# Attention values with the query on the output rows, half of the probabilities transposed on VectorE, and x parked in DRAM

## The chip, the core and the metric

The kernel runs on one core of a Trainium2 chip. The metric is the device time of one execution in microseconds, as the median of several executions. All arithmetic is in 32-bit floats. A core has TensorE (PE, matrix products into PSUM), VectorE (DVE), ScalarE (ACT), GpSimd (POOL) and SyncE (SP). In this kernel POOL, SP and ACT also issue DMA transfers. Each engine works through its own instructions in order; semaphores order the engines among one another.

## The reference, cut to what matters

x is 32 batches of 32 tokens with 512 features. Four layers each add their result to x; the last one takes most of the time:

```python
x = x + einsum('bct,bcd->bdt', x, weights[condition])                 # layer 0: mix tokens
x = x + einsum('bsi,oi->bso', x, W) + low_rank(x, lora_A, lora_B)*.5   # layer 1
x = x + einsum('bsi,boi->bso', x, weight[adapter_ids])                 # layer 2
# layer 3: attention, 32 query heads, 8 key heads, head size 128
q, k, v = x @ Wq.T, x @ Wk.T, x @ Wv.T
q, k = rope(rmsnorm(q)), rope(rmsnorm(k))
k_all = concat(k_cache[block_table], k); v_all = concat(v_cache[block_table], v)  # 512 + 32 keys
probs = softmax(where(valid, q @ k_all.T / sqrt(128), -1e30))
x = x + (probs @ v_all) @ Wo.T
```

Each batch has 512 cached keys (16 pages of 32, gathered by a table) and 32 new ones.

## The kernel before, in words

**First part.** Layers 0 to 2 run in tiles of 128 rows (four batches, eight tiles `t`). The running x stays in SBUF in `xs` to the end of the kernel. The projections follow: 12 chunks `c` of 512 output columns (8 of q, 2 of k, 2 of v) times 8 tiles, four 128-deep matmuls each (L295). q and k are normed, rotated (L315 to L341), turned by 32x32 blocks on DVE (L348) and stored by SP to `q_d` and `k_d`; v goes by way of ACT to `v_d`. The output weights `wo` (8 MB) are loaded by SP in four transfers during chunks 3 to 6. They have head size on the partitions: `wo[:, h, :]` is the block of head `h`.

**Attention.** A unit is a batch `b` and a key head `g`: 256 units, in the order of b and then g. Its four query heads times 32 tokens fill the 128 partitions. Four units of a batch are a quad. The order of all five engines' instructions is written out by hand in one loop over steps `n`; what follows lists the stages of a unit and the step at which each stands.

- Scores, step n: two matmuls against 288 and 256 keys (L673, L674) into one PSUM tile of two banks, which has a single buffer. DVE then adds the mask, takes each row's minimum and writes SBUF (`pr`, L680), which releases the PSUM tile.
- Exponential, step n: ACT raises `pr` and sums each row in `den` (L687).
- Division, step n+1: DVE takes 1/den (L692) and multiplies the 512 cached columns (L696). ACT does that of the 32 new columns into `pq` (L700).
- Flip, step n+2: four PE transposes (L707) turn the probabilities so that keys lie on the partitions, and ACT copies them out of PSUM into `pt` (L709).
- Values, step n+3: four matmuls with the value page as the stationary operand and `pt` as the moving one (L743), so that the output has head size on the partitions and queries along the columns.
- Once per quad: the four units' new-key probabilities are transposed together (L731, ACT copy L733), and four 32-row products per quad add the new values (L755, eight instructions). DVE copies the quad's output to `ot` (L765). The output PSUM tile takes four banks and has one buffer.
- Late units: the first unit of a quad, from batch 4 on and but for one (55 in all), takes another way. ACT divides it (L694), and DVE turns it with sixteen transposes of 32x128 each (L721), four in each of the steps n+3 to n+6. Its values follow at n+7.

**Output projection.** Batch tile `t` gives 32 blocks (L777, one head each), which are spread over the 32 steps of the next tile by the list `SHARE`: in steps 32 to 255 most have one, some two or none. Then DVE adds `xs` (L785) and SP stores. The last tile's blocks come at the end.

**Loads.** At g = 0 of batch b SP loads the new keys, the queries and the 16 key pages of batch b+1; at g = 4 POOL loads its 16 value pages. Both fill the buffers of batch b-1. The last two v projections (`FILL = 2`) are interleaved with the first steps of attention.

## Time and profile before

| what | value |
|---|---|
| median of 3 runs | 1284.76 us (1284.72 to 1284.89) |
| the profiled execution, its time | 1285.19 us |
| its span in the trace | 1283.5 us |
| PE busy | 1264.7 us, 99% |
| DVE busy | 873.9 us, 68% |
| ACT busy | 604.9 us, 47% |
| POOL busy | 377.2 us, 29% |
| granted TensorE clock | 1.0 throughout |
| first score matmul, score matmul of step 32, of step 255 | 427.15, 508.78 and 1242.78 us |

In the profile an instruction is named by its line, its engine and its operation, and the tiles that it writes and reads stand as `out<-in`. A fp32 matmul appears as two instructions, a PE transpose as one. A group's columns are its busy time, the mean duration of one in ns, and the idle time of the engine just before, with what ended it. Matmuls are pipelined and their ends are modelled, so a matmul's cost is better read from the start of one to the start of the next than from its duration. A wait of PE can show in the weight load (PEld) that comes ahead of the matmul.

### The profile page before, as it was taken

The page shows a single profiled execution, that of the slowest core. Times are in us where ns is not written, and L with a number is a line of the kernel's source. Part 1 is how long each engine was busy: PE and PEld are TensorE (multiplying, and loading weights), DVE is VectorE, ACT ScalarE, POOL GpSimd, SP SyncE. Part 2 cuts the span into 40 slices and gives each one's busy share as a digit, 9 for nine tenths or more (in the row PEclk, how much of TensorE's full clock was granted, in tenths as well). Part 3 has the DMA queues.
Part 4 walks back from the last instruction along what each step waited for, and adds up shares of the span by engine and source line. Part 5 has one row for each costly group of instructions (what it writes and reads, how often), then busy time and mean ns, then how long its engine had stood idle before and what let it go on. Part 6 is the DMA issues. An engine that isn't in the chain of part 4 may idle for free.

```text
span 1283.5 us, 23176 instructions
## 1 busy us (share of the span) xinstructions
PE 1264.7 (99%) x6284; PEld 827.9 (65%) x6284; DVE 873.9 (68%) x2515; ACT 604.9 (47%) x1625; POOL 377.2 (29%) x618
## 2 busy tenths in 40 slices
PE   8999999999999999999999999999999999999998
PEld 5444444444444688777777777777777777777774
DVE  3333767787881265688778778778877877887770
ACT  1232555555653466445445445545545544544540
POOL 2301533333342034223322333223322332222400
PEclk9999999999999999999999999999999999999999
DMA  8985755565458389866777586696677667758700
GB/s 335 426 341 182 203 134 174 172 180 166 118 144 236 122 234 240 222 181 188 180 216 199 157 207 188 167 237 185 194 196 195 193 175 203 207 152 217 192 25 9
DMA packets 176515, 246.69 MB, mean 192 GB/s; under 512 B 26209, under 2 KB 145377, under 8 KB 170114
## 3 DMA queue, kind: packets, MB, share of 16 engines
q1 hardware_dynamic: 147810, 163.25, 43.3%
q0 software_dynamic: 24832, 67.27, 20.2%
q10 hardware_dynamic: 3744, 14.68, 3.5%
q8 instruction: 52, 0.85, 0.3%
q14 instruction: 77, 0.63, 0.2%
HBM read 217.84 MB, written 27.26 MB: 191 GB/s over the span
## 4 chain that ended last, share of the span: by engine, by line
PE 89%; DVE 7%; DMA 2%; issue 1%; SPq 1%; ACT 0%; POOL 0%; DVEq 0%
PE qkv L295 26%; PE f_ps L777 18%; PE o_ps L743 16%; PE s_ps L673 8%; PE s_ps L674 7%; PE p_ps L707 6%; DVE pt L721 3%; PE o_ps L755 2%; DVE pr L680 2%; DMA wa<-in_w_adapt_dram 2%; PE adapt L483 2%; DVE pr L696 1%; PE base L463 1%; PE pn_ps L731 1%; PE base L464 0%
## 5 line engine op out<-in xcount | busy, mean ns | idle before, releaser
L184 POOL DMA_DIRECT2D vt<-in_v_cache_dram x480 | 240.7, 502 | 561.4 <-PE o_ps L743 409.8
L295 PE MATMUL qkv<-wq,x3t 128*128 128x512 f32 x768 | 331.8, 593 | 0.0
L680 DVE CUSTOM_DVE_ANT_0 pr<-s_ps,mask 128x544 f32<-128x544 f32 x256 | 185.5, 725 | 192.6 <-PE s_ps L674 187.1
L743 PE MATMUL o_ps<-pt,vt 128*128 128x128 f32 x2048 | 273.9, 277 | 9.2 <-DVE pt L721 9.1
L721 DVE STREAM_TRANSPOSE pt<-pr 32x128 f32<-32x128 f32 x880 | 265.8, 302 | 14.2
L743 PEld LDWEIGHTS o_ps<-pt,vt 128*128 128x128 f32 x2048 | 253.1, 192 | 22.0 <-DVE pt L721 17.6
L295 PEld LDWEIGHTS qkv<-wq,x3t 128*128 128x128 f32 x768 | 145.3, 190 | 183.2 <-issue 183.1
L709 ACT COPY pt<-p_ps 128x512 f32<-128x512 f32 x201 | 117.8, 586 | 302.8 <-PE p_ps L707 302.8
L777 PE MATMUL f_ps<-wo,ot 128*128 128x512 f32 x512 | 257.3, 605 | 0.0
L687 ACT ACTIVATE pr<-pr,low 128x544 f32<-128x544 f32 x256 | 192.1, 750 | 104.7 <-DVE low L680 103.2
L673 PE MATMUL s_ps<-kt,qt 128*128 128x288 f32 x512 | 170.4, 415 | 0.4 <-DVE low L680 0.4
L339 POOL TENSOR_TENSOR ra<-ra,rs 128x512 f32<-128x512 f32 x80 | 101.6, 1271 | 228.5 <-DVE rs L333 153.8
L673 PEld LDWEIGHTS s_ps<-kt,qt 128*128 128x128 f32 x512 | 92.1, 190 | 97.0 <-issue 77.2
L341 ACT ACTIVATE ra<-ra,rinv 128x128 f32<-128x128 f32 x320 | 102.2, 390 | 107.1 <-POOL ra L339 105.5
L674 PE MATMUL s_ps<-kt,qt 128*128 128x256 f32 x512 | 152.4, 379 | 0.2 <-issue 0.2
L707 PE MATMUL p_ps<-ident,pr 128*128 128x128 f32 x804 | 121.0, 273 | 0.0
L674 PEld LDWEIGHTS s_ps<-kt,qt 128*128 128x128 f32 x512 | 97.2, 190 | 27.4 <-issue 0.6
L707 PEld LDWEIGHTS p_ps<-ident,pr 128*128 128x128 f32 x804 | 99.9, 141 | 21.1 <-ACT pn L733 1.8
L777 PEld LDWEIGHTS f_ps<-wo,ot 128*128 128x128 f32 x512 | 82.3, 190 | 37.5 <-issue 30.6
L696 DVE TENSOR_SCALAR pr<-pr,rden 128x512 f32<-128x512 f32 x201 | 98.3, 489 | 7.2
L317 DVE TENSOR_REDUCE ss<-sq 128x4 f32<-128x512 f32 x80 | 53.8, 675 | 49.4 <-ACT sq L315 49.0
L700 ACT ACTIVATE pq<-pr,rden 128x32 f32<-128x32 f32 x256 | 78.7, 307 | 0.0
(91 smaller groups left out, 822.6 us busy)
## 6 DMA issues: line engine op xcount, KB each, us to landing
vt<-in_v_cache_dram POOLq DMA_DIRECT2D x512, 128.0 KB, 4.0
kt<-in_k_cache_dram SPq DMA_DIRECT2D x512, 128.0 KB, 3.9
wa<-in_w_adapt_dram SPq DMA_DIRECT2D x32, 1024.0 KB, 11.7
q_d<-st SPq DMA_DIRECT2D x256, 64.0 KB, 1.8
qt<-q_d SPq DMA_DIRECT2D x32, 512.0 KB, 5.8
wq<-in_w_qkv_dram ACTq DMA_DIRECT2D x10, 1024.0 KB, 5.3
wo<-in_w_o_dram SPq DMA_DIRECT2D x4, 2048.0 KB
k_d<-st SPq DMA_DIRECT2D x64, 64.0 KB, 2.0
```

Of the source, the lines that this page charges most:

```text
L184: self.eng.dma_start(out=out, in_=row)
L295: nc.tensor.matmul(ps, x3[:, k, :], w[:, k, :], start=(k == 0), stop=(k == KC - 1),)
L673: nc.tensor.matmul(ps[:, first:L], q, kt4[:, :N_LOW, g, :], start=True, stop=True)
L674: nc.tensor.matmul(ps[:, L : first + LT], q, kt4[:, N_LOW:, g, :], start=True, stop=True)
L680: nc.vector.tensor_tensor_reduce(pr, ps[:, first : first + LT], mask, -SCALE, 3.0e38, ALU.add, ALU.min, low)
L687: nc.scalar.activation(pr, pr, AF.Exp, bias=low, scale=-1.0, accum_out=den)
L696: nc.vector.tensor_scalar(pr[:, :L], pr[:, :L], rden, None, ALU.mult)
L707: nc.tensor.transpose(pp[:, c, :], pr[:, c * P : (c + 1) * P], ident)
L709: nc.scalar.copy(pt, pp)
L721: nc.vector.transpose(pt0s[b, g][j * S : (j + 1) * S, :, i * S : (i + 1) * S], blocks[:, :, j, :])
L743: nc.tensor.matmul(po[:, u, :P], vt[:, c, g * D : (g + 1) * D], pt[:, c, :], start=(c == 0), stop=False,)
L777: nc.tensor.matmul(pfs[t], ots[t, h // HALF][:, h % HALF, :], wo[:, h, :], start=(h == 0), stop=(h == HQ - 1),)
```

## The change

- Values are computed with the probabilities stationary and the value page moving, so that the output has queries on the partitions. The division therefore moves to the end of a quad: the exponentials stay undivided, and `keep` takes four reciprocals, multiplies the quad's 128x512 output from PSUM by them on DVE, and turns it by 32x32 blocks on DVE into `ot`.
- The rows of `ot` now hold (query head within the key head, d mod 32) and its columns' blocks (key head, d div 32). `wo` is loaded in that order, in 16 transfers to 32 partitions each in place of 4 to 128.
- The first quad of every batch takes no PE transposes. Each of its four units is turned by one DVE transpose of 128x512 in 32x32 blocks (`turn`, at g = 3 and 4 of the batch). Sixteen copies of 32x512 (`place`) then move the blocks to the right quarter of the partitions, four in each of the steps that start seven after the batch's first. Of each four, ACT makes 2, 2, 2, 4 for batches 0 to 2 and 1, 1, 1, 3 afterwards, and DVE the rest.
- The second quad of every batch is flipped on PE as before. The second quad's values come first: values of the batch's units 4 to 7 at the steps 7 to 10 after the batch's first, those of 0 to 3 at 11 to 14. The loop runs 7 steps beyond the last unit.
- ACT copies the new columns undivided. The late way is gone.
- x is stored to DRAM by POOL after the first part, and its SBUF is given back; the last addition loads a 256 KB tile of it by SP.
- Four v projections instead of two are interleaved, at steps 0, 1, 3 and 5. Value pages are loaded at g = 7 in place of 4, and the output blocks start three steps later, with heads 16 to 31 first.

```diff
-FILL = 2
+FILL = 4
+    x_d = dram.tile([NT, P, HID], F32, name="x_d")
...
+    nc.gpsimd.dma_start(out=x_d.rearrange("t p d -> p t d"), in_=xs)
+    first_part.close()
...
+    w_o4 = w_o.rearrange("(k d) (g r) o -> r k d g o", d=S, r=REP)
...
-            nc.sync.dma_start(out=wo[:, hs, :], in_=w_o[:, hs, :])
+            r = c - 3
+            for k in range(D // S):
+                nc.sync.dma_start(
+                    out=wo[r * S : (r + 1) * S].rearrange("d (g k) o -> d g k o", g=HK)[:, :, k, :],
+                    in_=w_o4[r, k],
+                )
...
+        nc.scalar.activation(
+            pr, pr, AF.Exp, bias=low, scale=-1.0, accum_out=dens[quad][:, u : u + 1]
+        )
+        nc.scalar.copy(news_p[quad][:, u, :], pr[:, L:])
...
+    def turn(b: int, us):
...
+        for u in us:
+            nc.vector.transpose(
+                turned[b][:, :, u, :, :].rearrange("p j c s -> p c j s"),
+                prs[b, 0].pop(u)[:, :L].rearrange("p (c j s) -> p c j s", j=P // S, s=S),
+            )
+    def place(b: int, i: int, on_act: int):
...
+        for j in range(P // S):
+            dst = placed[b][j * S : (j + 1) * S, :, :, i * S : (i + 1) * S]
+            src = turned[b][i * S : (i + 1) * S, j, :, :, :]
+            dst, src = (a.rearrange("p u c s -> p (u c) s") for a in (dst, src))
+            if j < on_act:
+                nc.scalar.copy(dst, src)
+            else:
+                nc.vector.tensor_copy(dst, src)
...
+        pt = pts.pop((b, g)) if q else placed[b][:, u, :, :]
         for c in range(L // P):
             nc.tensor.matmul(
                 po[:, u, :P],
+                pt[:, c, :],
                 vt[:, c, g * D : (g + 1) * D],
-                pt[:, c, :],
...
+        nc.vector.reciprocal(rden, dens.pop((b, q)))
+        o = tp.tile([P, QUAD, D], F32, tag="os", name=f"os_{b}_{q}", bufs=1)
+        nc.vector.tensor_tensor(
+            o, po[:, :, :P], rden.unsqueeze(2).to_broadcast([P, QUAD, D]), ALU.mult
+        )
+        nc.vector.transpose(
+            ots[t, q][:, :, j * S : (j + 1) * S],
+            o.rearrange("p u (k d) -> p (u k) d", d=S),
+        )
...
-        t, i = divmod(n - BT * HK, BT * HK)
+        t, i = divmod(n - 3 - BT * HK, BT * HK)
...
+    LAG = 7
+    ON_ACT = [[2, 2, 2, 4], [1, 1, 1, 3]]
+    FILLS = {0: NT - 4, 1: NT - 3, 3: NT - 2, 5: NT - 1}
...
-                if ahead_b and g == 4:
+                if g == 7 and 1 <= b < B - 1:
...
+            if 2 <= n < N + 2 and units[n - 2][1] >= QUAD:
+                flip(*units[n - 2])
+            if n < N:
+                exponentials(*scored)
+            if n in FILLS:
+                projected(NCH - 1, FILLS[n], 2)
+            if n < N and g in (3, 4):
+                turn(b, (0, 1) if g == 3 else (2, 3))
+            if n >= LAG and (n - LAG) % HK < QUAD:
+                bm, i = divmod(n - LAG, HK)
+                place(bm, i, ON_ACT[bm + 1 >= BT][i])
+            if n >= LAG:
+                bv, i = divmod(n - LAG, HK)
+                values(bv, (i + QUAD) % HK)
```

More of the change, by code (lines that the diff above doesn't have):

```diff
@@ L93, in cond_resid_kernel @@
     nc.vector.tensor_copy(pm, pm_m)
-    xs = const.tile([P, NT, HID], F32, name="xs")
-    intp = ctx.enter_context(ExitStack())
-    ii = intp.enter_context(tc.tile_pool(name="a_ii", bufs=1, side="right")).tile(
-        [P, N_INT], I32, name="ii"
-    )
+    first_part = ctx.enter_context(ExitStack())
+    xip = first_part.enter_context(tc.tile_pool(name="a_xi", bufs=1, side="right"))
+    xs = xip.tile([P, NT, HID], F32, name="xs")
+    ii = xip.tile([P, N_INT], I32, name="ii")
     nc.sync.dma_start(out=ii, in_=ints)
@@ L615, in cond_resid_kernel @@
             projected(0, NT - 1, 2)
-    intp.close()
+    nc.gpsimd.dma_start(out=x_d.rearrange("t p d -> p t d"), in_=xs)
+    first_part.close()
     flips.close()
@@ L632, in cond_resid_kernel @@
         if 3 <= c < 7:
-            hs = slice((c - 3) * HQ // 4, (c - 2) * HQ // 4)
-            nc.sync.dma_start(out=wo[:, hs, :], in_=w_o[:, hs, :])
+            r = c - 3
[4 more added lines that the diff above has]
+                )
         if c == (HQ + HK) // REP:
@@ L658, in cond_resid_kernel, with quad_of @@
     ots = {}
-    prs, pos = {}, {}
+    dens, news_p, prs, pos = {}, {}, {}, {}
     first = L - N_LOW * PSIZE
-    def late(b: int, g: int):
-        return g % QUAD == 0 and BT <= b and (b, g) != (B - 1, QUAD)
+    def quad_of(b: int, g: int):
+        return b, g // QUAD
     def scores(b: int, g: int):
@@ L676, in scores @@
         )
-        pr = tp.tile([P, LT], F32, tag="pr0" if late(b, g) else "pr", name=f"pr_{b}_{g}", bufs=2 if late(b, g) else 3)
+        pr = tp.tile([P, LT], F32, tag="pr", name=f"pr_{b}_{g}", bufs=4)
         low = tp.tile([P, 1], F32, tag="low", name=f"low_{b}_{g}", bufs=4)
@@ L685, in exponentials @@
     def exponentials(b: int, g: int, pr, low):
-        den = tp.tile([P, 1], F32, tag="den", name=f"den_{b}_{g}", bufs=4)
-        nc.scalar.activation(pr, pr, AF.Exp, bias=low, scale=-1.0, accum_out=den)
-        return b, g, pr, den
-    def divide(b: int, g: int, pr, den):
-        rden = tp.tile([P, 1], F32, tag="rden", name=f"rden_{b}_{g}", bufs=4)
-        nc.vector.reciprocal(rden, den)
-        if late(b, g):
-            nc.scalar.activation(pr[:, :L], pr[:, :L], AF.Copy, scale=rden)
-        else:
-            nc.vector.tensor_scalar(pr[:, :L], pr[:, :L], rden, None, ALU.mult)
-        quad = (b, g // QUAD)
-        if g % QUAD == 0:
-            prs[quad] = tp.tile([P, QUAD, S], F32, tag="pq", name=f"pq_{b}_{g}")
-        nc.scalar.activation(prs[quad][:, g % QUAD, :], pr[:, L:], AF.Copy, scale=rden)
-        return b, g, pr
@@ L703, in flip @@
-    def flip(b: int, g: int, pr):
+        quad, u = quad_of(b, g), g % QUAD
+        if u == 0:
+            dens[quad] = tp.tile([P, QUAD], F32, tag="den", name=f"den_{b}_{g}", bufs=4)
+            prs[quad] = {}
+            news_p[quad] = tp.tile([P, QUAD, S], F32, tag="pq", name=f"pq_{b}_{g}")
+        nc.scalar.activation(
+            pr, pr, AF.Exp, bias=low, scale=-1.0, accum_out=dens[quad][:, u : u + 1]
+        )
+        nc.scalar.copy(news_p[quad][:, u, :], pr[:, L:])
+        prs[quad][u] = pr
@@ new lines, in cond_resid_kernel @@
+    turned, placed = {}, {}
+    def turn(b: int, us):
+        if 0 in us:
+            turned[b] = tp.tile(
+                [P, P // S, QUAD, L // P, S], F32, tag="turned", name=f"turned_{b}", bufs=1
+            )
[5 more added lines that the diff above has]
+    def place(b: int, i: int, on_act: int):
+        if i == 0:
+            placed[b] = tp.tile(
+                [P, QUAD, L // P, P], F32, tag="placed", name=f"placed_{b}", bufs=1
+            )
[7 more added lines that the diff above has]
+                nc.vector.tensor_copy(dst, src)
@@ L705, in flip @@
+    pts = {}
+    def flip(b: int, g: int):
+        pr = prs[quad_of(b, g)].pop(g % QUAD)
         pp = ps_p.tile([P, L // P, P], F32, tag="p", name=f"p_ps_{b}_{g}")
@@ L707, in flip, with flip_new, values @@
             nc.tensor.transpose(pp[:, c, :], pr[:, c * P : (c + 1) * P], ident)
-        pt = tp.tile([P, L // P, P], F32, tag="pt", name=f"pt_{b}_{g}")
-        nc.scalar.copy(pt, pp)
-        return b, g, pt
-    pt0s = {}
-    def turn_part(b: int, g: int, pr, i: int):
-        if i == 0:
-            pt0s[b, g] = tp.tile([P, L // P, P], F32, tag="pt0", name=f"pt0_{b}_{g}", bufs=1)
-        blocks = pr[i * S : (i + 1) * S, :L].rearrange("p (c j k) -> p c j k", j=P // S, k=S)
-        for j in range(P // S):
-            nc.vector.transpose(
-                pt0s[b, g][j * S : (j + 1) * S, :, i * S : (i + 1) * S], blocks[:, :, j, :]
-            )
-    pns = {}
-    def flip_new(b: int, g: int):
-        quad = prs.pop((b, g // QUAD))
-        pnp = ps_p.tile([P, P], F32, tag="p", name=f"pn_ps_{b}_{g}")
-        nc.tensor.transpose(pnp, quad.rearrange("p u s -> p (u s)"), ident)
-        pns[b, g // QUAD] = tp.tile([P, P], F32, tag="pn", name=f"pn_{b}_{g}")
-        nc.scalar.copy(pns[b, g // QUAD], pnp)
-    def values(b: int, g: int, pt):
+        pts[b, g] = tp.tile([P, L // P, P], F32, tag="pt", name=f"pt_{b}_{g}")
+        nc.scalar.copy(pts[b, g], pp)
+    pns = {}
+    def flip_new(b: int, q: int):
+        pnp = ps_p.tile([P, P], F32, tag="p", name=f"pn_ps_{b}_{q}")
+        nc.tensor.transpose(pnp, news_p.pop((b, q)).rearrange("p u s -> p (u s)"), ident)
+        pns[b, q] = tp.tile([P, P], F32, tag="pn", name=f"pn_{b}_{q}", bufs=3)
+        nc.scalar.copy(pns[b, q], pnp)
+    def values(b: int, g: int):
         vt, vn = vts[b], vns[b]
         q, u = divmod(g, QUAD)
-        if (b, q) not in pos:
+        if u == 0:
             pos[b, q] = ps_o.tile([P, QUAD, L], F32, tag="o", name=f"o_ps_{b}_{g}")
         po = pos[b, q]
+        pt = pts.pop((b, g)) if q else placed[b][:, u, :, :]
         for c in range(L // P):
@@ L749, in values @@
             )
-        if u == (0 if late(b, q * QUAD) else QUAD - 1):
+        if u == QUAD - 1:
             pn = pns.pop((b, q))
@@ L754, in values @@
                 r = slice(i * S, (i + 1) * S)
-                nc.tensor.matmul(po[:, i, :P], vn[r, q, :], pn[r, :], start=False, stop=True)
-            return b, q
-        return None
+                nc.tensor.matmul(po[:, i, :P], pn[r, :], vn[r, q, :], start=False, stop=True)
+            keep(b, q)
     def keep(b: int, q: int):
@@ L762, in keep, with finish @@
         t, j = divmod(b, BT)
-        if j == 0:
+        if (t, q) not in ots:
             ots[t, q] = bp.tile([P, HALF, P], F32, tag="ot", name=f"ot_{t}_{q}")
-        nc.vector.tensor_copy(
-            ots[t, q][:, :, j * S : (j + 1) * S].rearrange("d (u r) s -> d u r s", u=QUAD),
-            po[:, :, :P].rearrange("d u (r s) -> d u r s", r=REP),
-        )
-    pfs = {}
-    def finish(t: int, hs):
-        for h in hs:
-            if h == 0:
+        rden = tp.tile([P, QUAD], F32, tag="rden", name=f"rden_{b}_{q}")
+        nc.vector.reciprocal(rden, dens.pop((b, q)))
+        o = tp.tile([P, QUAD, D], F32, tag="os", name=f"os_{b}_{q}", bufs=1)
+        nc.vector.tensor_tensor(
+            o, po[:, :, :P], rden.unsqueeze(2).to_broadcast([P, QUAD, D]), ALU.mult
+        )
+        nc.vector.transpose(
+            ots[t, q][:, :, j * S : (j + 1) * S],
+            o.rearrange("p u (k d) -> p (u k) d", d=S),
+        )
+    pfs, x3s = {}, {}
+    BLOCKS = list(range(HALF, HQ)) + list(range(HALF))
+    def finish(t: int, ns):
+        for n in ns:
+            h = BLOCKS[n]
+            if n == 0:
                 pfs[t] = ps_p.tile([P, HID], F32, tag="f", name=f"f_ps_{t}")
+                x3s[t] = tp.tile([P, HID], F32, tag="x3", name=f"x3_{t}", bufs=1)
+                nc.sync.dma_start(out=x3s[t], in_=x_d[t])
             nc.tensor.matmul(
@@ L780, in finish @@
                 wo[:, h, :],
-                start=(h == 0),
-                stop=(h == HQ - 1),
-            )
-            if h == HQ - 1:
-                nc.vector.tensor_tensor(xs[:, t, :], xs[:, t, :], pfs.pop(t), ALU.add)
-                nc.sync.dma_start(out=out[t * P : (t + 1) * P, :], in_=xs[:, t, :])
+                start=(n == 0),
+                stop=(n == HQ - 1),
+            )
+            if n == HQ - 1:
+                x3 = x3s.pop(t)
+                nc.vector.tensor_tensor(x3, x3, pfs.pop(t), ALU.add)
+                nc.sync.dma_start(out=out[t * P : (t + 1) * P, :], in_=x3)
     SHARE = [1, 2] * 5 + [1] + [1, 1, 1, 0] * 5 + [1]
     def share(n: int):
-        t, i = divmod(n - BT * HK, BT * HK)
+        t, i = divmod(n - 3 - BT * HK, BT * HK)
         if 0 <= t < NT - 1 and i < len(SHARE):
@@ L799, in cond_resid_kernel @@
     N = len(units)
-    scored, raised, divided, flipped, turned = [], [], [], [], []
+    LAG = 7
+    ON_ACT = [[2, 2, 2, 4], [1, 1, 1, 3]]
+    FILLS = {0: NT - 4, 1: NT - 3, 3: NT - 2, 5: NT - 1}
     order = {
@@ L808, in cond_resid_kernel @@
     with tc.manual_schedule(engines=order):
-        for n in range(N + 3):
+        for n in range(N + LAG):
+            b, g = divmod(n, HK)
+            at = B + (b + 1) * NPP
+            if n == max(FILLS) + 1:
+                pa.close()
+                bp = ctx.enter_context(tc.tile_pool(name="b_w", bufs=3))
+                ps_o = ctx.enter_context(tc.tile_pool(name="b_o", bufs=1, space=PSUM))
             if n < N:
-                b, g = units[n]
-                at = B + (b + 1) * NPP
-                ahead_b = 1 <= b < B - 1
-                if ahead_b and g == 0:
+                if g == 0 and 1 <= b < B - 1:
                     load_keys(b + 1)
@@ L819, in cond_resid_kernel @@
                     keys.transfer()
-                if ahead_b and g == 4:
+                if g == 7 and 1 <= b < B - 1:
                     values_in = Picked(nc.gpsimd, v_pages, at, page_values(b + 1), V_SHAPE)
                     values_in.transfer()
-                scored.append(scores(b, g))
-            if 2 <= n < N + 2:
-                if late(*units[n - 2]):
-                    turned.append((n + 1, divided.pop(0)))
-                else:
-                    flipped.append(flip(*divided.pop(0)))
@@ L830, in cond_resid_kernel @@
-            if n == FILL:
-                pa.close()
-                bp = ctx.enter_context(tc.tile_pool(name="b_w", bufs=3))
-                ps_o = ctx.enter_context(tc.tile_pool(name="b_o", bufs=1, space=PSUM))
-            if n < N:
-                raised.append(exponentials(*scored.pop(0)))
-            if 1 <= n <= N:
-                divided.append(divide(*raised.pop(0)))
+                scored = scores(b, g)
+            if 2 <= n < N + 2 and units[n - 2][1] >= QUAD:
+                flip(*units[n - 2])
@@ new lines, in cond_resid_kernel @@
+            if n < N:
+                exponentials(*scored)
[9 more added lines that the diff above has]
+                values(bv, (i + QUAD) % HK)
+                if i == HK - 1:
+                    placed.pop(bv), turned.pop(bv)
@@ L838, in cond_resid_kernel @@
+            if 2 <= n < N + 2 and (n - 2) % QUAD == QUAD - 1:
+                flip_new(units[n - 2][0], units[n - 2][1] // QUAD)
             if n < N and g == HK - 1 and b < B - 1:
                 see_keys(b + 1)
-            if n < FILL:
-                projected(NCH - 1, NT - FILL + n, 2)
-            if n == N:
-                finish(NT - 1, range(0, 4))
-            if n >= QUAD + 3 and late(*units[n - QUAD - 3]):
-                bu, gu = units[n - QUAD - 3]
-                keep(*values(bu, gu, pt0s.pop((bu, gu))))
@@ L849, in cond_resid_kernel @@
-            if n >= 3 and not late(*units[n - 3]):
-                if n == N - 1:
-                    share(n)
-                done = values(*flipped.pop(0))
-                if done is not None:
-                    keep(*done)
-            if turned and 0 <= n - turned[0][0] < QUAD:
-                at, unit = turned[0]
-                turn_part(*unit, n - at)
-                if n - at == QUAD - 1:
-                    turned.pop(0)
-            if 2 <= n < N + 2 and (n - 2) % QUAD == QUAD - 1:
-                flip_new(*units[n - 2])
@@ L862, in cond_resid_kernel @@
-            if n != N - 1:
-                share(n)
-            if n == N + 1:
-                finish(NT - 1, range(4, 11))
-        assert not scored and not raised and not divided and not prs and not pos
-        assert not flipped and not pns and not turned and not pt0s
-        finish(NT - 1, range(11, HQ))
+            share(n)
+            if n >= N + 3:
+                finish(NT - 1, range(3 * (n - N - 3), 3 * (n - N - 2)))
+        assert not dens and not news_p and not pos and not pts and not pns
@@ L872, in _laid_out @@
+        finish(NT - 1, range(12, HQ))
 def _laid_out(i):
```

## The prediction, made before the result was known

> **What bounds the kernel now.** I read the page's busy shares first.

> ```profile
> PE 1264.7 (99%) x6284; PEld 827.9 (65%) x6284; DVE 873.9 (68%) x2515; ACT 604.9 (47%) x1625; POOL 377.2 (29%) x618
> ```

> PE is the bound, but 99% hides waits, since modelled ends run into the next start. The table of stages shows where another engine comes close (columns: stretch, its length, then busy time and instructions of PE, PEld, DVE, ACT, POOL, then clock and DMA).

> ```profile
> 128.61:427.15 298.54, 298.54 (x696) 132.08 (x696) 201.33 (x445) 155.64 (x460) 108.11 (x103) 1.00 0.62 173
> 427.15:508.78 81.63, 81.24 (x560) 67.92 (x559) 46.63 (x136) 49.93 (x133) 22.74 (x46) 1.00 0.75 187
> 613.80:719.30 105.50, 104.16 (x617) 78.93 (x616) 83.19 (x262) 52.00 (x136) 32.17 (x64) 1.00 0.72 193
> 1242.78:1283.50 40.72, 36.84 (x141) 19.67 (x139) 6.14 (x15) 4.14 (x11) 0.00 (x0) 0.99 0.04 13
> ```

> The projections are pure PE time. The third row is four batches of steady attention: 105.5 us, DVE at 79%. Then the PE timeline inside it, read start to start:

> ```profile
> 703.35 0.60 PE L707 MATMUL p_ps<-ident,pr 128*128 128x128 f32 x4
> 704.22 1.16 PE L743 MATMUL o_ps<-pt,vt 128*128 128x128 f32 x8 [0.27 <-DVE pt L721]
> 705.31 0.50 PE L755 MATMUL o_ps<-pn,vn 32*128 32x128 f32 x8
> 705.74 1.12 PE L777 MATMUL f_ps<-wo,ot 128*128 128x512 f32 x2
> 706.70 0.65 PE L673 MATMUL s_ps<-kt,qt 128*128 128x288 f32 x2
> ...
> 707.62 0.60 PE L707 MATMUL p_ps<-ident,pr 128*128 128x128 f32 x4
> 708.06 1.06 PE L743 MATMUL o_ps<-pt,vt 128*128 128x128 f32 x8
> 708.95 1.02 PE L777 MATMUL f_ps<-wo,ot 128*128 128x512 f32 x2
> 709.81 0.65 PE L673 MATMUL s_ps<-kt,qt 128*128 128x288 f32 x2
> ```

> Prices on PE: scores 0.92 (706.70 to 707.62), a flip 0.44, a unit's values 0.89, an output block 0.86, the new values of a quad 0.53 (0.43 here and 0.10 ahead), and 0.10 more on the block behind them. The second line shows the hidden wait: values due at 703.79 start at 704.22 and run 0.10 longer, so 0.53 lost to DVE. Last, the groups by form:

> ```profile
> L721 DVE STREAM_TRANSPOSE pt<-pr 32x128 f32<-32x128 f32 x880 | 265.8, 302 | 14.2
> L743 PEld LDWEIGHTS o_ps<-pt,vt 128*128 128x128 f32 x2048 | 253.1, 192 | 22.0 <-DVE pt L721 17.6 <-issue 1.0 <-DVE ot L765 0.6
> ...
> L348 DVE STREAM_TRANSPOSE st<-ra 128x512 f32<-128x512 f32 x80 | 55.8, 699 | 5.2 <-DMA k_d<-st 2.2 <-POOL ra L339 1.3 <-DMA q_d<-st 1.2
> L323 DVE TENSOR_TENSOR ra<-qkv,cw 128x512 f32<-128x512 f32 x80 | 54.8, 685 | 4.7 <-DVE st L348 0.5
> ...
> L511 ACT ACTIVATE nsn<-ang 128x512 f32<-128x512 f32 x1 | 0.6, 612 | 0.0
> ...
> L503 DVE TENSOR_SCALAR turns<-ang 128x512 f32<-128x512 f32 x1 | 0.4, 426 | 0.0
> ```

> 880 transposes are 55 late units of 16; 35 of these make PE wait, 17.6 us by the weight loads.

> [...] four L721 take 1.25 to 1.26 us at 302 each, so they don't overlap. [...]

> **The change, part by part.**

> *Removed from PE.* 201 units flip now (804 transposes); afterwards only second quads do, 128. 73 x 0.44 = 32.1 us. The operand swap costs nothing: same shapes, same instruction count. The late units' waits go: 35 x 0.53 = 18.6.

> *DVE's new work* per batch: 8 score passes at 0.73 start to start, 4 turns at 0.70 (L348), 10 copies at 0.43 (L503; bounds 0.43 and 0.69[...]; I take 0.43[...]), two ends of a quad at 0.17 + 0.69 + 0.70, the mask 0.50: 5.8 + 2.8 + 4.3 + 3.1 + 0.5 = 16.5 of some 25 us. The removed divisions (489 + 158 ns a unit) pay for it. It stays covered by PE, but where it stands matters. After its scores end, a step's DVE pass starts 0.20 later and frees the scores' PSUM 0.78 after that: a gap of 0.98 on PE, which every step with values and one block (1.75) covers; the six steps in 32 without a block have 1.0 to 1.4. I put 0.2 per four batches there: 1.4.

> *ACT and the new wait.* A 32x512 copy from SBUF is 0.61 (L511[...]). In the step with the last four copies, counted from the end of its scores: exponential at 0.20 + 0.85, new columns 0.75 later, three copies from 1.92 to 3.57, seen by PE at 3.6. PE has values 0.89, new values 0.53, one block 0.96, next scores 0.92: ready at 3.30 for the first quad's values, which need all sixteen copies. It waits 0.3 and pays 0.1 for unprefetched weights. Behind the wait stand that step's block and the next scores, hence the next DVE pass. Where `SHARE` has two blocks (one batch in four) nothing waits. 28 x 3/4 x 0.4 = 8.4. Bounds: nothing if ACT's copies run nearer 0.4, far more if runs of 32 elements slow them.

> *Batches 0 to 3*, without output blocks to cover anything. PE's work is 17.5 per batch (now 19.6). But with four copies on ACT the last ends at 4.1 where PE is ready at 2.3: 1.9 lost, plus some 0.6 in gaps below 0.98: 20.0. Walking it: first scores at 420.3 (two projections of 3.43 later), steps 0, 1, 3, 5 of 4.35, steps 2, 4, 6 of 1.9 (as 435.85 to 437.75 now), step 7 at 443.4, three batches to 503.4, step 35 at 512.6, with 0.7 more in the wait there. It is at 519.7 now, but the new order then still owes four units of values (3.6) and four blocks (3.4): 520.3. So the 16 flips saved by then (7.0 of the 32.1) come back, with 0.6 more: 7.6.

> *Tail.* Same PE work; the blocks of heads 16 to 31 cover the last quad's 1.6 us on DVE. 0. If not, at most 2.

> *Loads.* Storing x on POOL: 2 MB in 1024 pieces; the indirect gathers take 990 ns for 128 rows, so I estimate up to 8 us of POOL. Cover: POOL is busy 108 of 298 us there, three `ra` buffers and six accumulators of 3.43 us each stand between it and PE. `wo`: twelve more issues[...]; the stores of q and k queue behind it on SP, with the same cover, and `wo` is needed 200 us later. Uncovered, either costs under 10 us. Loading x on SP waits for the last store; behind it are the keys of a batch five steps (15 us) later. Value pages move three steps back, but so does their use: 16 issues of 0.93 and 4.0 landing are 19 us in a window of 27 (22 early). All 0.

> Sum, on the profiled span: 1283.5 - 32.1 - 18.6 + 1.4 + 8.4 + 7.6 = 1250.2. The profiled execution was 1.7 above its span and 0.4 above the median: 1251.5.

> **Rivals.** *No new waits*: ACT and DVE deliver the copies in time and the early batches keep their gain: 16.0 less, 1235.5. For it: ACT is busy half the time. Against: the last four copies follow an exponential of the same step. [...]copies of 0.69 end 0.44 after the next DVE pass is due, in the step without a block, and push the exponential and the wait behind it: 21 x 0.44 = 9.2, some 3 early: 1264; with unoverlapped ACT copies (3 x 0.09 x 21, 0.9 a batch early) 1272. For it: no row shows such a copy to strided runs. *Slower: ACT's quarter-crossing copies.* Each 0.1 us on one adds 0.3 to 28 batches and 1.0 to 3.5 early ones, 11.9 in all; 33 us are gone at 0.81 us a copy instead of 0.52. At twice the price, 1311. For it: ACT writes only contiguous runs so far.[...]

> **How the numbers follow.** Forecast 0.58 (1244 to 1261), no new waits 0.16, slower DVE copies 0.16, slow ACT copies 0.10, of which 0.03 land within 0.2% of before, about what a measurement of this kernel can tell from no change. Faster 0.90, same 0.03, slower 0.07. The range goes from the second case to the top of the third: 1236 to 1273.

> **What would show it.** 512 transposes on L707's successor; no wait of PE on a DVE transpose; in three batches of four a wait of 0.3 to 0.5 on ACT's `placed` ahead of the first quad's values; four batches in some 100.6 us; ACT copies near 612 ns, DVE copies near 430; step 35 near 513. ACT copies above 0.8 us, DVE near 90% busy, or PE waiting for value pages would make it wrong.

## The result, and the profile after

The changed kernel takes 1298.67 us (median of 4 runs, 1297.12 to 1300.91) against 1284.83 for the kernel before, a ratio of 1.0108 with a 95% interval of 1.009 to 1.0125: 1.1% slower, where 1251.5 us was forecast. The profiled execution took 1300.91 us with a span of 1299.2 us, 49.0 us more than the span of 1250.2 that the sum gave.

The busy shares of the changed kernel first, as the page gives them:

```profile
PE 1247.2 (96%) x5992; PEld 799.5 (62%) x5992; DVE 762.2 (59%) x1742; ACT 661.9 (51%) x1701; POOL 382.0 (29%) x619
```

PE has 292 instructions fewer (73 units of four flips), and DVE is busy 112 us less. But PE is at 96%, no longer 99%: it waits. The table of stages says where (columns as before: the stretch, its length, busy time and count of PE, PEld, DVE, ACT and POOL, the clock, the DMA share, GB/s). The rows are the projections, the steps 0 to 35, and four batches of steady attention:

```profile
128.61:447.24 318.63, 304.09 (x686) 133.28 (x685) 201.51 (x445) 156.43 (x458) 108.99 (x105) 0.96 0.64 165
447.24:550.84 103.60, 90.83 (x526) 70.06 (x524) 57.74 (x136) 69.32 (x165) 21.99 (x45) 0.97 0.65 169
645.08:747.00 101.92, 99.79 (x585) 74.84 (x584) 65.12 (x150) 57.70 (x146) 32.49 (x65) 1.00 0.86 202
```

Steady attention gained (101.9 us where it had 105.5). The projections, which the sum took as they were, lost: PE stands still for 14.5 us in them (318.63 less 304.09), and the clock falls to 0.96. Against the terms of the sum:

| part | forecast, us | measured, us | difference |
|---|---|---|---|
| up to the first scores | 420.3 | 447.24 | +26.9 |
| steps 0 to 35 | 93.0 | 103.60 | +10.6 |
| steps 35 to 255 | 692.1 | 702.85 | +10.8 |
| from step 255 to the end | 44.8 | 45.51 | +0.7 |

The first two forecasts are the prediction's own walk. The last two split what is left of its sum, and were worked out from the two traces afterwards: at step 255 the new order still owes three units of values and two blocks more than the old one (4.4 us), less a wait of the late way that falls away there (0.3).

**The projections.** PE's timeline there (start, length, engine, line, then the instructions run together, and in brackets the wait ahead of the first):

```profile
226.21 29.40 PE L296 MATMUL qkv<-wq,x3t 128*128 128x512 f32 x64 [3.63 <-DVE rs L334]
259.25 30.57 PE L296 MATMUL qkv<-wq,x3t 128*128 128x512 f32 x64 [3.63 <-DVE rs L334]
293.46 30.53 PE L296 MATMUL qkv<-wq,x3t 128*128 128x512 f32 x64 [3.64 <-DVE rs L334]
327.62 119.78 PE L296 MATMUL qkv<-wq,x3t 128*128 128x512 f32 x272 [3.63 <-DVE rs L334]
```

Four equal waits, 64 instructions (one chunk of eight tiles) apart, for a product of the rotation on DVE (L334), which is the last reader of an accumulator in PSUM. DVE's timeline ahead of the first of them:

```profile
219.87 0.69 DVE L318 TENSOR_REDUCE ss<-sq 128x4 f32<-128x512 f32 x1 [2.75 <-ACT sq L316]
223.30 0.69 DVE L318 TENSOR_REDUCE ss<-sq 128x4 f32<-128x512 f32 x1 [2.75 <-ACT sq L316]
...
224.71 0.69 DVE L324 TENSOR_TENSOR ra<-qkv,cw 128x512 f32<-128x512 f32 x1
...
225.65 0.41 DVE L334 TENSOR_TENSOR rs<-qkv,sw 128x256 f32<-128x256 f32 x1
```

DVE is not busy. It stands in its own order, idle for 2.75 us and again for 2.75 us, for the row sums of two tiles whose squares ACT has not yet made, because PE has only just computed them. Behind those sums stands the rotation that would free the accumulator PE needs next. The projections are not in an order written by hand, as attention is: a planner puts each engine's instructions in order when the program is built. It ordered DVE's rows differently in the two kernels. This is the listing of DVE's instructions in program order in chunk 4 (row, line, operation, the tile number as the first figure), ahead of the second wait, for the kernel before:

```
296 L317 TensorReduce ss_7<-sq_7 128x4
297 L348 StreamTranspose st_3<-ra_3 128x4x4x32
298 L323 TensorTensor ra_6<-qkv_6,cw 128x512
```

and for the changed kernel, at the same tiles (the serial numbers behind the tile are left out in both):

```
288 L318 TensorReduce ss_7<-sq_7 128x4
289 L318 TensorReduce ss_0<-sq_0 128x4
290 L318 TensorReduce ss_1<-sq_1 128x4
291 L349 StreamTranspose st_1<-ra_1 128x4x4x32
292 L324 TensorTensor ra_4<-qkv_4,cw 128x512
```

Tiles 0 and 1 are those of the next chunk. In chunk 3, which the timeline shows, the changed kernel's order is the same. With (4,4) standing for chunk 4, tile 4: the six accumulators hold (4,4) to (5,1), PE cannot start (5,2) before the rotation of (4,4) has read its accumulator, and DVE will not do that rotation before it has summed (5,0) and (5,1). So PE runs dry once in each of four chunks, as many as there are with `wo` transfers.

The waits come to 14.5 us. Most of the rest is the clock. The table of windows for the ten microseconds behind the second wait, in two parts:

```profile
259.25:265.02 5.77, 5.77 (x7) 2.49 (x8) 4.15 (x10) 2.55 (x8) 3.15 (x3) 0.50 0.56 134
265.02:269.00 3.98, 3.98 (x10) 1.71 (x9) 2.38 (x5) 1.95 (x6) 0.64 (x1) 1.00 0.22 54
```

PE is busy throughout, but at half its clock for 5.8 us and then at the full one. Behind the third and fourth wait it runs at half for 5.7 us each, and behind the first for 3.4: 1.7, 2.9, 2.9 and 2.8 us less work, 10.3 together. It shows in the sum as well: the L296 matmuls are busy 343.2 us, and in an experiment below, without these waits, 332.1. So each of the four waits of 3.63 us was followed by a low clock. The last section comes back to this, with shorter ones.

**The copies and the turns.** The changed kernel's groups by form, columns as before:

```profile
L763 PE MATMUL o_ps<-vt,placed 128*128 128x128 f32 x1024 | 139.7, 280 | 20.3 <-ACT placed L730 20.3
...
L732 DVE COPY placed<-turned 32x512 f32<-32x512 f32 x308 | 132.2, 429 | 6.3
...
L730 ACT COPY placed<-turned 32x512 f32<-32x512 f32 x204 | 125.5, 615 | 2.0
```

Durations are as forecast: DVE's copies 429 ns, ACT's 615, 512 transposes on PE (L741), and no PE wait on a DVE transpose. What is more than forecast is the 20.3 us on `placed`. Of it 6.0 are three early waits of 2.0, in batches 0 to 2. The other 14.3 are one wait of 1.50, in batch 3, and 20 of 0.64 or 0.65 in later batches. One of the 20 on PE's timeline, in a step whose scores ended at 831.13:

```profile
835.23 1.16 PE L763 MATMUL o_ps<-vt,placed 128*128 128x128 f32 x8 [0.64 <-ACT placed L730]
```

ACT's timeline in such a step (its scores ended at 883.54 on PE) shows how they come about. This step has two output blocks, so PE itself came later and didn't wait; ACT's times after the end of the scores are the same in the steps that wait:

```profile
884.62 0.75 ACT L698 ACTIVATE pr<-pr,low 128x544 f32<-128x544 f32 x1 [1.17 <-DVE low L687]
885.27 0.19 ACT L698 ACTIVATION_READ_ACCUMULATOR pr<-pr,low 128x1 f32 x1
885.49 0.22 ACT L701 COPY pq<-pr 128x32 f32<-128x32 f32 x1
885.72 1.87 ACT L730 COPY placed<-turned 32x512 f32<-32x512 f32 x3
```

From the end of the scores: exponential at 1.08, new columns at 1.95, copies from 2.18 to 4.05. The sum had the copies from 1.92 to 3.57: 0.61 for the first and 0.52 for each of the two others, which puts an overlap of 0.09 between them. In the trace before, four activations of 128x128 show such an overlap: they take 0.39 each (the mean of all 320 of L341), but 1.28 together, not 1.56.

```profile
304.43 1.28 ACT L341 ACTIVATE ra<-ra,rinv 128x128 f32<-128x128 f32 x4
```

That copies of 32x512 would overlap in the same way was an assumption, and no row of the trace before shows it. Three of them take 1.87, or 0.62 each; they do not overlap.

In batches 0 to 2 the same queue makes PE wait three times a batch. The longest of the three on PE's timeline, ahead of the first values of batch 1's first quad:

```profile
507.25 1.99 PE L763 MATMUL o_ps<-vt,placed 128*128 128x128 f32 x8 [2.00 <-ACT placed L730]
```

Values wait 2.00 us, and then the eight matmuls take 1.99 us where they took 1.06 at full clock. Some six and four microseconds earlier in each of these batches the new keys' transpose (L750) waits 0.9 us and the new values (L775) 0.5, because ACT's copy of a flip (L743) stands behind the two `place` copies of that step.

### The profile page after: what moved, and what is told of

Its sections match the earlier page's. It is cut to its first block, busy times and chain, and to the rows that moved or that the text cites. A ratio compares the mean times of both kernels' runs of the same rounds, so it can differ in the third digit from the quotient of the medians.

```text
span 1299.2 us, 22028 instructions
## 1 busy us (share of the span) xinstructions
PE 1247.2 (96%) x5992; PEld 799.5 (62%) x5992; DVE 762.2 (59%) x1742; ACT 661.9 (51%) x1701; POOL 382.0 (29%) x619
## 4 chain that ended last, share of the span: by engine, by line
PE 82%; ACT 10%; DMA 3%; DVE 3%; issue 2%; SPq 1%; POOL 0%; DVEq 0%; ACTq 0%
PE qkv L296 26%; PE f_ps L808 16%; PE o_ps L763 15%; PE s_ps L680 8%; PE s_ps L681 7%; ACT placed L730 4%; PE p_ps L741 4%; ACT pr L698 3%; PE adapt L484 2%; DMA wa<-in_w_adapt_dram 2%; DVE pr L687 1%; PE o_ps L775 1%; PE base L464 1%; ACT pq L701 1%; ACT pt L743 0%
## 5 line engine op out<-in xcount | busy, mean ns | idle before, releaser
L185 POOL DMA_DIRECT2D vt<-in_v_cache_dram x480 | 244.8, 510 | 553.1 <-PE o_ps L763 361.9
L296 PE MATMUL qkv<-wq,x3t 128*128 128x512 f32 x768 | 343.2, 608 | 14.5 <-DVE rs L334 14.5
L296 PEld LDWEIGHTS qkv<-wq,x3t 128*128 128x128 f32 x768 | 148.8, 195 | 204.5 <-issue 204.3
L763 PE MATMUL o_ps<-vt,placed 128*128 128x128 f32 x1024 | 139.7, 280 | 20.3 <-ACT placed L730 20.3
L743 ACT COPY pt<-p_ps 128x512 f32<-128x512 f32 x128 | 75.0, 586 | 159.9 <-PE p_ps L741 159.6
L763 PEld LDWEIGHTS o_ps<-vt,placed 128*128 128x128 f32 x1024 | 131.1, 194 | 36.9 <-ACT placed L730 32.1
L732 DVE COPY placed<-turned 32x512 f32<-32x512 f32 x308 | 132.2, 429 | 6.3
L763 PE MATMUL o_ps<-vt,pt 128*128 128x128 f32 x1024 | 135.1, 275 | 0.0
L763 PEld LDWEIGHTS o_ps<-vt,pt 128*128 128x128 f32 x1024 | 126.8, 192 | 1.6
L730 ACT COPY placed<-turned 32x512 f32<-32x512 f32 x204 | 125.5, 615 | 2.0
L714 DVE STREAM_TRANSPOSE turned<-pr 128x512 f32<-128x512 f32 x128 | 83.2, 688 | 3.0 <-ACT placed L730 3.0
```

Of the source, the lines that this page charges most:

```text
L185: self.eng.dma_start(out=out, in_=row)
L296: nc.tensor.matmul(ps, x3[:, k, :], w[:, k, :], start=(k == 0), stop=(k == KC - 1),)
L730: nc.scalar.copy(dst, src)
L732: nc.vector.tensor_copy(dst, src)
L763: nc.tensor.matmul(po[:, u, :P], pt[:, c, :], vt[:, c, g * D : (g + 1) * D], start=(c == 0), stop=False,)
```

## The experiments

All ratios are to the kernel before, measured on the same chip alongside. Theories in short: the projections lose because of *the 16 narrow transfers of* `wo`, by the order they bring about or by their own slowness; or because of *x's store and the rest of the change*; the rest of the loss is *ACT's last copies*.

### wo_full: the changed kernel with `wo` laid out beforehand

The rows and columns of `w_o` are put in the new order in what is handed to the kernel, so that it comes in 4 transfers to 128 partitions. The rearrangement itself is left out of the kernel; all else is the changed kernel.

```diff
-            r = c - 3
-            for k in range(D // S):
-                nc.sync.dma_start(
-                    out=wo[r * S : (r + 1) * S].rearrange("d (g k) o -> d g k o", g=HK)[:, :, k, :],
-                    in_=w_o4[r, k],
-                )
+            hs = slice((c - 3) * HQ // 4, (c - 2) * HQ // 4)
+            nc.sync.dma_start(out=wo[:, hs, :], in_=w_o[:, hs, :])
```

> The changed kernel with one thing undone: the output weights are laid out beforehand in the order that the new outputs need, and loaded as in the kernel before, by four transfers to 128 partitions. Theory A (the sixteen 32-partition transfers make the planner put DVE's row sums of two or three later tiles ahead of the transposes and rotations of an earlier one, and PE runs out of accumulators): the four PE waits of 3.63 us in the projections and the low clock behind them go, the first scores start near 420.3 us instead of 447.2, and the time falls by 27 us to about 1272. Theory B (the transfers themselves hold up the stores on SP): the same here. Theory C (storing x from POOL delays the projections): the first scores stay near 447 and the time near 1298.

Measured 1273.97 us (1273.01 to 1274.28), ratio 0.9915 (0.9898 to 0.9931). Its table of stages, projections and steps 0 to 35:

```profile
128.61:419.88 291.27, 291.27 (x680) 128.86 (x679) 201.06 (x445) 153.63 (x457) 108.90 (x105) 1.00 0.63 178
419.88:524.59 104.71, 91.94 (x526) 71.12 (x524) 57.74 (x136) 69.32 (x165) 21.93 (x45) 0.95 0.66 169
```

PE is busy in the whole of the first row, and the first scores come at 419.88, where the forecast had 420.3. The transfers of `wo` account for all of the loss in the projections; x's store has none in it. What remains over the forecast is in the early and the steady batches (104.7 and 702.6 us; the changed kernel has 103.6 and 702.9).

### before_wo16: the kernel before with the 16 transfers

Its output projection keeps the old row order, and the sources are divided as in the changed kernel (2 KB runs to 32 partitions).

```diff
-            hs = slice((c - 3) * HQ // 4, (c - 2) * HQ // 4)
-            nc.sync.dma_start(out=wo[:, hs, :], in_=w_o[:, hs, :])
+            r = slice((c - 3) * S, (c - 2) * S)
+            for k in range(D // S):
+                nc.sync.dma_start(
+                    out=wo[r].rearrange("d (g k) o -> d g k o", g=HK)[:, :, k, :],
+                    in_=w_o[r].rearrange("d (g k) o -> d g k o", g=HK)[:, :, k, :],
+                )
```

> The kernel before with one thing added: its output weights, in its own order, come in sixteen transfers to 32 partitions each, in runs of 2 KB, at the same places as in the changed kernel. Theories A and B: four PE waits of some 3.6 us appear in chunks 3 to 6, first scores near 454 us instead of 427.15, time near 1311. Theory C: no change, 1285.

Measured 1309.7 us (1307.82 to 1312.09), ratio 1.019 (1.0173 to 1.0207). First scores at 453.96 in place of 427.15: 26.8 us, about as much as the changed kernel has over wo_full (27.4). Everything after it takes the time it took (from step 255 to the end 41.0 against 40.7). Its list of waits (engine and line, what it waits for, total us, times, longest):

```profile
PE qkv L295 <- DVE rs L333: 14.5, 4, 3.6
```

The same four waits. In program order DVE has `ss_7`, `ss_0`, `ss_1`, `st_1`, `ra_4` here too. So neither the values, the copies, the freed SBUF nor the store of x is needed for the loss.

### wo16_128 and wo16_long: which property of the transfers it is

Both start from wo_full. The first has 16 transfers in runs of 2 KB, but to 128 partitions; the second has 16 to 32 partitions in runs of 16 KB.

```diff
 # wo16_128
-            hs = slice((c - 3) * HQ // 4, (c - 2) * HQ // 4)
-            nc.sync.dma_start(out=wo[:, hs, :], in_=w_o[:, hs, :])
+            for k in range(4 * (c - 3), 4 * (c - 2)):
+                nc.sync.dma_start(
+                    out=wo.rearrange("p (g k) o -> p g k o", g=2)[:, :, k, :],
+                    in_=w_o.rearrange("p (g k) o -> p g k o", g=2)[:, :, k, :],
+                )
 # wo16_long
-            hs = slice((c - 3) * HQ // 4, (c - 2) * HQ // 4)
-            nc.sync.dma_start(out=wo[:, hs, :], in_=w_o[:, hs, :])
+            r = slice((c - 3) * S, (c - 2) * S)
+            for k in range(4):
+                hs = slice(k * HQ // 4, (k + 1) * HQ // 4)
+                nc.sync.dma_start(out=wo[r, hs, :], in_=w_o[r, hs, :])
```

> As wo_full, but the weights come in sixteen transfers of 512 KB to all 128 partitions, in runs of 2 KB, at the places of the changed kernel. If the narrow target is what matters (32 partitions, to the planner and on the chip): no stall in the projections, first scores near 420 us, 1274. If the number of transfers or the short runs matter: the four waits come back, first scores near 447, 1298.

> As wo_full, but in sixteen transfers of 512 KB to 32 partitions each, in runs of 16 KB instead of the changed kernel's 2 KB. If the narrow target is what matters: four PE waits of 3.6 us as in the changed kernel, first scores near 447, about 1298. If the short runs matter: near 420 and 1274.

wo16_128 took 1274.43 us, ratio 0.9915 (0.9898 to 0.9931), with no wait on L296 and that line busy for 332.1 us. wo16_long took 1297.17 us, ratio 1.009 (1.0073 to 1.0107), with 14.5 us in four waits on L334 and DVE's order as in the changed kernel. The number of transfers and the length of a run change the time by 1.5 us at most; that a transfer goes to 32 partitions does it. DVE's order in chunks 3 to 6 is the same in the three kernels with a planned order and narrow transfers (the changed one, before_wo16 and wo16_long), and without them it is another one, in the kernel before, wo_full, wo16_128 and the two kernels further below with fewer copies on ACT. That the planner takes a narrow transfer to be slow, expects the stores behind it and with them the `st` buffers to be late, and therefore moves the transposes and what follows them back, fits all this, but is not shown.

### dve_by_hand and hand_full: order and transfers apart

For chunks 2 to 9 DVE keeps the order in which the program issues its instructions, tile by tile, with the reciprocal moved behind the products of the rotation. dve_by_hand keeps the narrow transfers, hand_full has those of wo_full.

```diff
-        rinv = tp.tile([P, REP], F32, tag="rinv", name=f"rinv_{c}_{t}")
-        nc.vector.reciprocal(rinv, rms)
...
+        rinv = tp.tile([P, REP], F32, tag="rinv", name=f"rinv_{c}_{t}")
+        nc.vector.reciprocal(rinv, rms)
         nc.gpsimd.tensor_tensor(a, a, s, ALU.add)
...
-        for t in range(1 if c == 1 else 0, NT if c < NCH - 1 else NT - FILL):
+        with tc.manual_schedule(engines={mybir.EngineType.DVE}) if 2 <= c < 10 else nullcontext():
+            for t in range(1 if c == 1 else 0, NT if c < NCH - 1 else NT - FILL):
```

> The changed kernel with all its transfers, but with DVE's order in chunks 2 to 9 of the projections written by hand: for each tile the row sum, the three rotation products, the reciprocal, then the transpose of the tile two earlier. Theory A (the order is what stalls PE): no wait of 3.6 us, first scores near 421, time near 1272. Theory B (the transfers delay the stores on the chip): the stalls stay, near 1298, or come back as DVE waits for its store buffers.

> DVE's order of dve_by_hand together with the four 128-partition transfers of wo_full. If the 12 us that dve_by_hand still lost in the projections are the narrow transfers' delay of the stores: DVE's waits for its store buffers go, first scores near 420, about 1274. If the hand-written order itself costs them: first scores near 432, about 1285.

dve_by_hand took 1285.51 us (1282.82 to 1289.02), ratio 1.0001 (0.9987 to 1.0016); hand_full 1272.27 us (1271.9 to 1272.65), ratio 0.9898 (0.9881 to 0.9914). From the list of waits of dve_by_hand:

```profile
DVE st L349 <- DMA q_d<-st: 41.8, 9, 6.5
...
PE qkv L296 <- DVE rinv L339: 9.9, 6, 3.3
```

and of hand_full, where PE has no wait on L296 for DVE:

```profile
DVE st L349 <- DMA q_d<-st: 15.3, 8, 4.4
```

Each of the two theories, A (the order) and B (the transfers' own slowness), has half of the loss. With the narrow transfers in place, DVE's order by hand gives back 13.2 us (1298.67 to 1285.51), where theory A expected all of it back (1272) and theory B nothing (1298). ACT's order in the projections, which the planner still makes, moved along with DVE's, so this half belongs to the two together. The other half is the transfers themselves: DVE waits up to 6.5 us for the store of an earlier tile, which stands behind the `wo` transfers in SP's queue, and PE runs dry for 9.9 us. The longest time from issue to landing of such a store is 11.7 us in the changed kernel and in dve_by_hand, 7.8 in hand_full, 7.5 in the kernel before. Without the narrow transfers another 13.2 us go (to 1272.27). Both halves need the narrow transfers; in wo_full, where they are gone, the planned order costs only 1.7 us over that by hand.

### on_act_fewer and on_act_split: ACT's last copies

Both are wo_full with fewer of the copies on ACT, and DVE taking the others: of the last four copies of an early batch two, or one, in place of four; of a later batch one, or two, in place of three. on_act_split also has one instead of two in the other steps of the early batches.

```diff
-    ON_ACT = [[2, 2, 2, 4], [1, 1, 1, 3]]
+    ON_ACT = [[2, 2, 2, 2], [1, 1, 1, 1]]   # on_act_fewer
+    ON_ACT = [[1, 1, 1, 1], [1, 1, 1, 2]]   # on_act_split
```

> As wo_full, and ACT makes only one of the last four copies of a batch (two in batches 0 to 2) instead of three (four); DVE makes the others. Theory D (PE's wait ahead of the first quad's values is ACT's queue: exponential, new columns and three copies of 0.62 us one after the other): the last copy of ACT ends at 2.8 us after its step's scores instead of 4.05, PE is ready at 3.3, so the waits of 0.75 us in steady batches go (19 us) and those of 2.2 in the early ones halve (some 7 us with the low clock): about 1246. Theory E (DVE then becomes late, since its end of a quad follows two copies more): PE waits for the scores' DVE pass instead, and no more than half is gained: 1255 to 1265.

> As wo_full, with ACT making 1, 1, 1, 1 of the copies in batches 0 to 2 and 1, 1, 1, 2 afterwards. By the queue lengths measured so far: in steady batches ACT's two copies end 2.18 + 1.24 = 3.4 us after their step's scores, PE is ready at 3.3, so 0.1 to 0.2 is lost instead of the 0.35 that DVE's second copy cost through the next scores; in the early batches ACT reaches the flip's copy in time, so the waits of 1.1 us there shrink. 1248 to 1255, against 1256.6 for on_act_fewer. If DVE is late in the early batches instead, no gain.

on_act_fewer took 1256.56 us (1255.61 to 1258.47), ratio 0.9783 (0.9767 to 0.98), and on_act_split 1251.96 us (1250.69 to 1252.83), ratio 0.9743 (0.9726 to 0.9759), the fastest of all. From the list of waits of on_act_fewer:

```profile
PEld s_ps L675 <- DVE low L682: 9.8, 30, 1.2
...
PE o_ps L758 <- ACT placed L725: 2.3, 3, 0.8
```

PE's waits on `placed` fall from 20.3 to 2.3 us, so they were ACT's (theory D). But 17.4 us are gained and not the 28 that D alone promised: the rest moves to the other engine, as theory E had it. The scores' weight loads now wait 9.8 us for DVE's pass, 30 times, where they did so 3 times for 2.9 us in the changed kernel. The stages of on_act_split, four steady batches and steps 0 to 35:

```profile
732.67:832.68 100.01, 99.75 (x585) 74.93 (x584) 66.51 (x154) 55.23 (x142) 32.96 (x65) 1.00 0.85 206
419.59:514.74 95.15, 88.18 (x525) 67.27 (x524) 65.24 (x154) 58.02 (x147) 22.77 (x45) 1.00 0.68 184
```

With one copy more on ACT, four steady batches take 0.4 us less than in on_act_fewer (100.0 against 100.4). Steps 0 to 35 fell from 104.7 to 98.0 and then to 95.2 us, their clock rose from 0.95 to 1.00, and with one copy a step the waits of the new keys' transpose for ACT are gone; instead PE waits three times, 3.1 us together, for DVE's end of a quad. Of the 23.3 us between the spans of wo_full (1272.4) and on_act_split (1249.0), 9.6 are in these steps, and 13.5 in steps 35 to 255 (702.6 to 689.1); the rest of the kernel is the same within 0.3. So all of it came from taking copies out of ACT's queue, and part of the early gain is the clock that came back with it.

## Why the prediction was wrong

**The step that failed** is in "Loads": `wo`, "the stores of q and k queue behind it on SP, with the same cover", "All 0". The narrow transfers did take longer than the wide ones: the four pieces of a chunk took 13.3 to 14.2 us from the first issue to the last landing (in the three chunks for which the trace has it), where the 2 MB of wo_full took 8.1 to 8.4. Behind them a store of q or k took up to 11.7 us to land; in wo16_128, with as many pieces of the same size, but to 128 partitions, up to 7.5. The cover was misjudged. I counted three `ra` buffers and six accumulators of 3.43 us each, 20.6 us between a store and PE, as if DVE could work on whatever was ready. But DVE works in one order; a stalled transpose, or an early row sum, holds up the rotation that frees the accumulators. And I took that order as given, when it is made anew for every program: half of the loss comes from an order, and no row of the profile before could show it. My "uncovered, either costs under 10 us" was too low as well: with the order by hand the transfers alone cost 13.2 us, with the planned one 24.7 (1298.67 against 1273.97). This is 26.9 of the 49.0 us. Without it the change is 0.85% faster.

**ACT and the new wait.** Place and cause were right: before the first quad's values, for `placed`, in three batches of four. The size was off. PE's side, ready at 3.30 after the end of the scores, was right: with two blocks the values start at 4.15, one block (0.86) later. In the 20 steps with one block they start at 4.10, so 0.80 us is lost in each rather than 0.3 (the profile shows 0.64 of it as idle time, since the modelled ends run over). Of the 10.8 us of the steady part, 20 x 0.5 = 10.0 are this. ACT's last copy ended at 4.05 rather than 3.57. The larger wrong term is the overlap of 0.09, which L341 shows in the trace before and these copies mostly don't have: it is missing ahead of the first copy (which begins 0.23 behind the new columns' start, not 0.12) and between the three (1.87, not 1.65), 0.33 us in all. The other 0.15 is the start of the new columns at 1.95 rather than 1.80: behind the exponential stands a read of its row sums of 0.19, which the sum left out.

**Batches 0 to 3** had 93.0 us and took 103.6. The walk put three batches at 20.0 each, from the scores of step 7 to those of step 31; they took 22.3, 24.0 and 24.0. The 1.9 at the last copy is nearly right (2.0). Missing were two waits for ACT's copies of a flip and of the new keys, 1.4 us a batch together, and the clock: the second and third batch lost another 1.7 each, as much as 3.41 us at half the clock cost (507.37 to 510.78 in the second). on_act_split took 95.2 for these steps.

**The rivals.** The slower rival, ACT's quarter-crossing copies, has its first tenth in the result (0.62 for 0.52, which it priced at 11.9 us: the missing overlap of 0.09); its point of decision, 0.81, was not reached, and it isn't why the kernel became slower. The rival of slower DVE copies, at 0.69 us, fell: they took 429 ns. "No new waits" fell with the waits of 20.3 us for `placed`.

**What held.** 73 flips less; no matmul's wait on a DVE transpose (weight loads of scores stand behind a turn 15 times, 3.6 us in all); the operand swap free (a unit's values take 0.89 us from start to start, 838.01 to 838.90, as before); x's store harmless (wo_full, first scores at 419.88), the load of x and the value pages too (PE itself waits for no DMA in attention); the tail within 0.7 us. The steady part did fall by 20.2 us, 723.1 to 702.9, where 31.0 was forecast.

## What to carry to other kernels

When a change touches a transfer that shares a queue with stores, ask not only whether there is time enough until the data are used, but which instruction waits for the stores behind it and what stands behind that instruction in its engine's order. Where a planner makes the order, look at the new program's order in stages that the change doesn't touch; a different target shape of one transfer moved DVE's work there. And when work is moved to a second engine, add what is queued ahead of it in the same step: the split of copies that looked harmless by the share of busy time (ACT at 51%) was worth 22 us.

## What the runs showed of the hardware beside this

This tells two equal waits apart. The wait of 2.00 us ahead of the values at 507.25 lies whole in one window, and these values ran at half the clock. That ahead of the values at 484.86, a batch earlier, is as long but split over two windows, in which PE is busy for 67% and 59%, and there the clock stayed up. The rows are the second of these two windows, the one before 507.37, and the one behind it:

```profile
483.47:486.89 3.42, 2.03 (x14) 1.88 (x15) 1.78 (x4) 2.37 (x6) 0.00 (x0) 1.00 0.41 119
503.95:507.37 3.42, 1.42 (x13) 0.80 (x6) 2.17 (x5) 3.32 (x8) 0.98 (x2) 1.00 1.09 224
507.37:510.78 3.41, 3.41 (x12) 3.00 (x13) 1.16 (x2) 0.91 (x3) 0.00 (x0) 0.50 1.10 222
```

So of two waits of 2.00 us one was followed by a low clock and one was not; in this trace the share of a window in which PE was idle tells them apart, and the length of the wait does not. This is read from one trace; no run was made to test it.
